# Out-projection ahead of the scores in every slot of a fused attention and feed-forward block

## The chip, the cores and the metric

The kernel runs on one core of a Trainium2 chip. The metric is the device time of one execution in microseconds; the time before is the median of three runs. The chip's engines have short names here, as in the profile: PE is TensorE (matmuls; PEld are its weight loads), DVE is VectorE, ACT is ScalarE, POOL is GpSimd, and SP is the engine whose queue issues most DMAs. Each engine works through its own instructions in the order in which they were written down, and waits at an instruction until the semaphores that it names have arrived.

## The reference

One transformer block on x of shape (2, 1024, 256), all in fp32. A small modulation gives each batch entry a shift, a scale and a gate for both halves of the block. Cut to what matters here:

```python
h = layernorm(x) * (1 + ca) + sa
q, k, v = h @ Wq + bq, h @ Wk + bk, h @ Wv + bv      # 16 heads of 128
q, k = rotary(q * 128 ** -0.5), rotary(k)
attn = softmax(causal(q @ k.T))                      # 1024 x 1024 for each batch entry and head
x = x + ga * ((attn @ v) @ Wo + bo)
h = layernorm(x) * (1 + cb) + sb
x = x + gb * ffn(h)                                  # silu(gate) * up, down; hidden size 704
```

## The kernel before

The attention is a loop over 32 **units** (2 batch entries x 8 head groups x 2 heads), numbered 0 to 31 by `n`, and in each unit over 8 **slots** `i`, one for each block of 128 query rows. The whole order is written out by hand (`tc.manual_schedule()`): each engine executes its instructions in the order in which this loop names them, and only semaphores tie the engines together.

In slot i of a unit the kernel computes, for query block i:

- `score` (L380): one or two fp32 matmuls per block, (i+1) x 128 columns wide in all, from `qT` and `kT` into the PSUM tile `ps` (L392). Every fp32 matmul appears as two passes in the trace. Then one DVE instruction adds the causal mask and finds the negative row maximum `nmax` (L395, with a second short row that reads the accumulator).
- `turned` (L422): DVE transposes the exponentials of the slot **before** (i-1) in 32x32 squares into `t32` (L426). Slot 0 does so for the last block of the unit before. After blocks 3 and 7, SP issues 16 DMAs (L438) that move the squares into `pT`, the transposed probabilities of four blocks.
- `expo` (L407): ACT computes exp(ps - max) from PSUM and the row sums `den` (L412).
- `project_out` (L472): for an earlier unit whose attention output `o` is complete, one matmul of 256 columns, `py` (L479), and on DVE the sum of x, x = py * rden + x (L482). In slots 0 to 3 it takes rows 4 to 7 of unit n-2, in slots 4 to 7 rows 0 to 3 of unit n-1. In slots 0 and 4 a reciprocal of four row sums (L476) stands ahead of it on DVE.
- `release` (L375): the second half of a rotary embedding (L365 on DVE, L368 on POOL) of a projection that was made in the slot before.
- One more piece of TensorE work: in slots 1, 3, 4 and 6 a projection of q or k for the next unit (`project_qk`, L349; ACT's L361 and POOL's L362 follow), in slots 0 and 2 a projection of v (`project_v`, L331, copied out of PSUM by ACT), in slots 5 and 6 `values` (L453), the product with v of blocks 4 to 7 of the unit before, and in slot 7 the same for blocks 0 to 3 of this unit.
- `extras` (L545): small pieces that belong to certain units, such as layer-norm statistics (units 13 and 28), the scaling and turning of normalised rows by TensorE transposes (L201, L210, L217; units 14, 15, 30, 31) and scaling of feed-forward weights.

In unit 31, which has no next unit, slots 1 to 6 carry matmuls of the feed-forward (`hidden`, L508) in place of projections. After the loop come the last out-projections and the rest of the feed-forward.

What matters for the order is which buffers each piece shares. PSUM is divided among `ps` (two buffers, `ps_sc`), `py` (**one** buffer, `ps_y`), `po` (one buffer, `ps_o`) and the projections (two buffers, `ps_a`). A matmul into a buffer waits until the last reader of what lay in it is done: `py` waits for the L482 before it, `ps` for the exponential two slots back, `po` for ACT's copy of `o`. `pT` has one buffer for each half of a unit; its copies wait for the `po` matmuls that read the last contents, and `po` waits for the copies to land.

Of the kernel before, what the change touches and what calls it, by code (L numbers as in the profile page):

```python
# [37 lines left out]
def adaln_block(ctx: ExitStack, tc: tile.TileContext, a, cos_d, sin_d, out):  # L38
# [24 lines left out]
    def load_x(b, t, n, eng):  # L63
        eng.dma_start(x[b][:, t : t + n, :], x_d[b, :, t : t + n, :])
# [123 lines left out]
    def ln_sqrt(b, name, t0, t1):  # L188
        mv, rstd = stats[b, name]
        nc.scalar.activation(rstd[:, t0:t1], mv[:, t0:t1, 1], AF.Sqrt, bias=eps_t)  # L190
# [79 lines left out]
    def new_hT(b, blk):  # L270
        hT[b, blk] = hpool.tile([P, KC, QB], F32, tag=f"hT{blk}", name=f"hT{b}_{blk}")
        return hT[b, blk]

    def load_w(b, g, n):
        t = wpool.tile([P, KC, HG * DH], F32, tag=f"w{n}", name=f"w{n}_{b}{g}")
        nc.sync.dma_start(
            t, a[f"L0_attn_W{n}"][g]
        )
        weights[b, g][n] = t

    def load_proj(b, g):
        weights[b, g] = {}
        for n in ("q", "k", "v"):
            load_w(b, g, n)

    def load_out(b, g):
        t = wpool.tile([P, HG, D], F32, tag="wo", name=f"wo_{b}{g}")
        nc.sync.dma_start(
            t, a["L0_attn_Wo"][g]
        )  # L290
        weights[b, g]["o"] = t
# [88 lines left out]
    def score(u, i):  # L380

        b, g, h = u
        tag = f"{b}{g}{h}{i}"
        qT, kT = qks[u, "q"], qks[u, "k"]
        L = (i + 1) * P
        if i == 0:
            dens[u] = small.tile([P, NT], F32, tag="den", name=f"den_{tag}", bufs=3)
            rdens[u] = small.tile([P, NT], F32, tag="rden", name=f"rden_{tag}", bufs=3)
        ps = ps_sc.tile([P, S], F32, tag="sc", name=f"ps_{tag}")
        for c in range(0, L, 512):  # L390
            e = min(L, c + 512)
            nc.tensor.matmul(ps[:, c:e], qT[:, ts(i, P)], kT[:, c:e], start=True, stop=True)  # L392

        nmax = small.tile([P, 1], F32, tag="nmax", name=f"nmax_{tag}")
        nc.vector.tensor_tensor_reduce(  # L395
            ps[:, :L],
            ps[:, :L],
            mask[:, NT - 1 - i :, :].rearrange("p t k -> p (t k)"),
            -SCALE,
            FLT_MAX,  # L400
            ALU.add,
            ALU.min,
            nmax,
        )
        return ps, nmax
# [60 lines left out]
    def bank(name):  # L466

        pool, tag = banks[turn[0] % 4]
        turn[0] += 1
        return pool.tile([P, 512], F32, tag=tag, name=name)  # L470

    def project_out(u, t, late=False):  # L472

        b, g, h = u
        if t % 4 == 0:
            nc.vector.reciprocal(rdens[u][:, t : t + 4], dens[u][:, t : t + 4])  # L476
        name = f"py_{b}{g}{h}{t}"
        py = bank(name) if late else ps_y.tile([P, 512], F32, tag="y", name=name)
        nc.tensor.matmul(  # L479
            py[:, :D], outs[u][:, ts(t, P)], weights[b, g]["o"][:, h, :], start=True, stop=True  # L480
        )
        nc.vector.scalar_tensor_tensor(  # L482
            x[b][:, t, :], py[:, :D], rdens[u][:, t : t + 1], x[b][:, t, :], ALU.mult, ALU.add
        )
# [57 lines left out]
    units = [(b, g, h) for b in range(B) for g in range(NG) for h in range(HG)]  # L542
# [52 lines left out]
    with tc.manual_schedule():  # L595
        nc.scalar.activation(
            sc.rearrange("p b k -> p (b k)"), sc.rearrange("p b k -> p (b k)"), AF.Silu
        )
        nc.scalar.activation(warm, eps_t, AF.Sqrt)
        weights[0, 0] = {}  # L600
        load_w(0, 0, "q")
        load_w(0, 0, "k")
        for t, t_d in ((cos_t, cos_d), (sin_t, sin_d)):
            nc.sync.dma_start(t[:, :QB], t_d[:, :QB])
        load_w(0, 0, "v")
        for t in (4, 6):
            load_x(0, t, 2, nc.sync)
        for t, t_d in ((cos_t, cos_d), (sin_t, sin_d)):
            nc.sync.dma_start(t[:, QB:], t_d[:, QB:])
        nc.sync.dma_start(wga, a["w_gates"])  # L610
        nc.sync.dma_start(wmod[:, 1], a["L0_wmod"][1])
        load_proj(*units[2][:2])
        load_out(0, 0)
        nc.gpsimd.memset(bvacc, 0.0)

        for blk, t in enumerate(t32):
            for j in range(3):
                nc.gpsimd.memset(t[:, :, j, 4 * blk + j + 1 :, :], 0.0)
        for t in (0, 2):
            for j in range(2):  # L620
                ln_stats(0, "a", t + j)
            ln_sqrt(0, "a", t, t + 2)
            if t:
                ln_scale(0, "a", 0, (0, 1))
        modulation(0, ps_y, "y")
        ln_scale(0, "a", 0, (2, 3))
        shift_scale(0)
        ln_turn(0, "a", 0, 0, new_hT(0, 0), split=True)
        for t in range(4, NT):
            ln_stats(0, "a", t)  # L630
        ln_sqrt(0, "a", 4, NT)
        for s in ("q", "k"):
            project_qk(units[0], s, 0)
        for t in (0, 2):
            project_v(0, 0, t, *((ps_o, "o"), (ps_y, "y"))[t // 2])
        ln_scale(0, "a", 1)
        release()
        ln_turn(0, "a", 1, 0, new_hT(0, 1), split=True)
        gates()
        for s in ("q", "k"):  # L640
            project_qk(units[0], s, 1)
        nc.gpsimd.dma_start(bo_bc, a["L0_attn_bo"].to_broadcast([P, D]))

        for n, u in enumerate(units):
            b, g, h = u
            prev = units[n - 1] if n else None
            nxt = units[n + 1] if n + 1 < N else None
            nb, ng = (b, g + 1) if g + 1 < NG else (b + 1, 0)
            more = nb < B
            for i in range(NT):  # L650
                ps, nmax = score(u, i)
                if i >= 1:
                    turned(u, i - 1)
                elif prev:
                    turned(prev, NT - 1)
                expo(u, i, ps, nmax)

                if i < 4 and n > 1:
                    project_out(units[n - 2], 4 + i)
                if i >= 4 and prev:  # L660
                    project_out(prev, i - 4)
                release()
                if i in (1, 3, 4, 6) and nxt:
                    project_qk(nxt, *{1: ("q", 0), 3: ("k", 0), 4: ("q", 1), 6: ("k", 1)}[i])
                if i in (5, 6) and prev:
                    values(prev, 1, 4 * (i - 5), 4 * (i - 4))

                if i == 7 and prev:
                    values(u, 0, 0, 4)
                if n == 1 and i == 1:  # L670
                    values(prev, 0, 0, 4)
                if i in (0, 2):
                    if h == 0:
                        project_v(b, g, 4 + i)
                    elif more:
                        project_v(nb, ng, i)
                if not nxt and 1 <= i < 7:
                    hidden(0, 0, i - 1, late=False)
                extras(n, i)
                if i == 7 and h == 1:  # L680
                    if more:
                        load_out(nb, ng)
                    if n + 3 < N:
                        load_proj(*units[n + 3][:2])

        u, prev = units[-1], units[-2]
        turned(u, 7)
        for c in range(4):
            hidden(0, 1, c)
            project_out(prev, 4 + c, late=True)  # L690
            project_out(u, c, late=True)
        values(u, 1, 0, 8)
        hidden(0, 1, 4)
        for t in range(4, NT):
            project_out(u, t, late=True)
        hidden(0, 1, 5)
        for t in range(NT):
            ln_stats(1, "b", t)
        ln_sqrt(1, "b", 0, NT)
        down(0, 0, 0)  # L700
        ln_scale(1, "b", 0)
        down(0, 0, 1)
        down(0, 0, 2)
        ln_turn(1, "b", 0, 2, new_h2(1, 0))
        down(0, 0, 3)
        ln_scale(1, "b", 1)
        for c in range(NF):
            hidden(1, 0, c)
            if c == 0:
                ln_turn(1, "b", 1, 2, new_h2(1, 1))  # L710
            if c in (1, 2, 3, 4):
                down(0, 1, c - 1)
        for c in range(NF):
            hidden(1, 1, c)
            if c in (1, 2, 3, 4):
                down(1, 0, c - 1)
        for j in range(4):
            down(1, 1, j)
# [68 lines left out]
```

## Time and profile before

| What | Value |
|---|---|
| Median of 3 runs | 1104.93 us (1104.89 to 1105.02) |
| The profiled execution: its time / its span | 1106.62 us / 1104.9 us |
| Granted TensorE clock over the span | 0.998 |
| PE `ps` L392, `po` L453, `py` L479: busy, instructions | 289.7 us x768, 263.3 us x768, 157.2 us x512 |
| DVE maximum L395, transpose L426, sum of x L482: busy, instructions | 195.7 us x256, 198.2 us x256, 115.9 us x256 |
| ACT exponential L412: busy, instructions | 189.7 us x256 |
| `pT` copies L438 on SP's queue: issues of 128 KB and of 64 KB | x512, x512 |

How to read it: the span runs from the first to the last instruction of the profiled execution; the execution's own time has a little around it. A group's row gives busy time, count and mean duration. A row of the timeline gives the start in us from the span's start, the duration in us, then engine, line, operation and tiles; "[0.35 <-DVE x L482]" at its end is the idle time of the engine before it and what ended it. A row "xN" merges N neighbours, and its duration runs from the first one's start to the last one's end. Matmuls are pipelined, so the row of one is longer than the distance to the next. In a table of waits, a row names who waited for whom, the total in us, how often, and the longest. A row of the table by stretches gives the stretch, its length, the busy time and count of PE, PEld, DVE, ACT and POOL, the granted TensorE clock (1.00 is full), the share of the DMA engines and GB/s.

### The profile page before, as it was taken

How to read it: one execution, taken by the hardware profiler on the slowest of the kernel's cores; microseconds unless marked ns; L12 is line 12 of the kernel's file. 1: busy time of each engine (PE TensorE's matmuls, PEld its weight loads, DVE VectorE, ACT ScalarE, POOL GpSimd, SP SyncE). 2: the span in 40 equal slices, each digit the busy share in tenths (PEclk: the TensorE clock that was granted, in tenths of full speed). 3: DMA queues.
4: the chain of work that ended last, by engine and by line, in shares of the span. 5: the costliest groups of instructions: out<-in, count | busy, mean ns of one | idle time of the engine just before them, and what ended most of it. 6: DMA issues, size and time to landing. Idle time of an engine off the chain costs nothing.

```text
span 1104.9 us, 12352 instructions
## 1 busy us (share of the span) xinstructions
PE 1092.1 (99%) x3556; PEld 645.3 (58%) x3556; DVE 643.0 (58%) x1406; ACT 508.5 (46%) x953; POOL 391.8 (35%) x356
## 2 busy tenths in 40 slices
PE   9999999999999999999999999999999999999998
PEld 5555555555666565555555656656565555455555
DVE  5556565666566666865566566555656757544311
ACT  5644444554555445354454455444444454641110
POOL 4635353535353433444333543333433433000000
PEclk9999999999999999999999999999999999999999
DMA  6365656556556655265654546454545455331000
GB/s 213 83 146 126 162 117 167 144 119 146 127 144 143 146 112 134 65 145 115 142 125 110 143 110 145 108 143 109 139 101 139 97 118 115 85 79 32 24 19 29
DMA packets 65656, 128.88 MB, mean 117 GB/s; under 512 B 18451, under 2 KB 22803, under 8 KB 65589
## 3 DMA queue, kind: packets, MB, share of 16 engines
q1 hardware_dynamic: 63236, 123.81, 47.5%
q10 hardware_dynamic: 2304, 4.16, 1.1%
q8 instruction: 29, 0.48, 0.2%
q14 instruction: 39, 0.31, 0.1%
q0 software_dynamic: 48, 0.13, 0.1%
HBM read 25.26 MB, written 2.10 MB: 25 GB/s over the span
## 4 chain that ended last, share of the span: by engine, by line
PE 97%; DVE 3%; issue 0%; ACT 0%; POOL 0%; DVEq 0%; ACTq 0%; POOLq 0%
PE ps L392 22%; PE po L453 22%; PE py L479 10%; PE pq L349 10%; PE pk L349 10%; PE pv L331 9%; PE pgu L508 7%; PE pd L530 4%; DVE t L426 1%; PE warm_ps L82 1%; DVE ps L395 1%; PE pm L119 0%; PE ptx_a L210 0%; DVE x L482 0%; DVE kT L365 0%
## 5 line engine op out<-in xcount | busy, mean ns | idle before, releaser
L395 DVE CUSTOM_DVE_ANT_0 ps<-ps,mask 128x128 f32<-128x128 f32 (+7 forms) x256 | 195.7, 764 | 328.9 <-PE ps L392 328.5
L412 ACT ACTIVATE p<-ps,nmax 128x128 f32<-128x128 f32 (+7 forms) x256 | 189.7, 741 | 345.8 <-DVE nmax L395 342.4
L392 PE MATMUL ps<-kT,qT 128*128 128x512 f32 (+3 forms) x768 | 289.7, 486 | 0.7 <-ACT p L412 0.7
L453 PE MATMUL po<-pT,v 128*128 128x512 f32 (+3 forms) x768 | 263.3, 486 | 0.0
L392 PEld LDWEIGHTS ps<-kT,qT 128*128 128x128 f32 x768 | 140.9, 190 | 127.2 <-issue 120.8
L453 PEld LDWEIGHTS po<-pT,v 128*128 128x128 f32 x768 | 145.9, 190 | 115.4 <-issue 91.8
L426 DVE STREAM_TRANSPOSE t<-p 128x128 f32<-128x128 f32 (+7 forms) x256 | 198.2, 774 | 1.0 <-ACT p L412 0.7
L479 PE MATMUL py<-wo,o 128*128 128x256 f32 x512 | 157.2, 391 | 1.5 <-DVE x L482 1.5
L362 POOL TENSOR_TENSOR r_k<-r_k,sin_t 128x512 f32<-128x512 f32 x64 | 81.3, 1271 | 209.8 <-ACT r_k L361 209.7
L368 POOL TENSOR_TENSOR kT<-kT,r_k 128x512 f32<-128x512 f32 x64 | 81.5, 1273 | 162.7 <-DVE kT L365 148.3
L362 POOL TENSOR_TENSOR r_q<-r_q,sin_t 128x512 f32<-128x512 f32 x64 | 81.8, 1277 | 150.8 <-ACT r_q L361 147.1
L479 PEld LDWEIGHTS py<-wo,o 128*128 128x128 f32 x512 | 90.0, 190 | 61.2 <-issue 30.9
L331 PE MATMUL pv<-wv,hT 128*128 128x256 f32 x512 | 120.9, 379 | 1.1 <-DVE qT L365 1.1
L349 PE MATMUL pq<-hT,wq 128*128 128x512 f32 x256 | 120.6, 593 | 0.5 <-DVE hT L217 0.5
L482 DVE SCALAR_TENSOR_TENSOR x<-py,rden,x 128x256 f32<-128x256 f32 x256 | 115.9, 455 | 8.0 <-DVE rden L476 0.9
L349 PE MATMUL pk<-hT,wk 128*128 128x512 f32 x256 | 120.3, 592 | 0.0
L361 ACT ACTIVATE r_q<-pq,cols 64x512 f32<-64x512 f32 x128 | 87.4, 683 | 48.1 <-PE pq L349 47.2
L331 PEld LDWEIGHTS pv<-wv,hT 128*128 128x128 f32 x512 | 97.1, 190 | 15.2 <-DVE qT L365 1.2
L361 ACT ACTIVATE r_k<-pk,cols 64x512 f32<-64x512 f32 x128 | 87.4, 683 | 18.0 <-PE pk L349 15.9
L368 POOL TENSOR_TENSOR qT<-qT,r_q 128x512 f32<-128x512 f32 x64 | 83.7, 1308 | 25.3 <-DVE qT L365 20.7
L349 PEld LDWEIGHTS pk<-hT,wk 128*128 128x128 f32 x256 | 48.6, 190 | 35.8 <-issue 32.0
L349 PEld LDWEIGHTS pq<-hT,wq 128*128 128x128 f32 x256 | 48.3, 190 | 35.7 <-issue 31.2
(83 smaller groups left out, 704.6 us busy)
## 6 DMA issues: line engine op xcount, KB each, us to landing
pT<-t SPq DMA_DIRECT2D x512, 128.0 KB, 2.4
pT<-t SPq DMA_DIRECT2D x512, 64.0 KB, 2.0
wq<-in_Wq SPq DMA_DIRECT2D x16, 256.0 KB, 3.0
wk<-in_Wk SPq DMA_DIRECT2D x16, 256.0 KB, 4.1
wv<-in_Wv SPq DMA_DIRECT2D x16, 256.0 KB, 4.3
wo<-in_Wo SPq DMA_DIRECT2D x16, 256.0 KB, 2.9
out<-yo SPq DMA_DIRECT2D x16, 128.0 KB, 1.7
x<-in_x SPq DMA_DIRECT2D x4, 256.0 KB, 5.1
```

The costliest lines, as they stand in the source:

```text
L331: nc.tensor.matmul(pv[:, ts(j, HG * DH)], hT[b, n][:, k, ts(r, P)], weights[b, g]["v"][:, k, :], start=(k == 0), stop=(k == KC - 1),)
L349: nc.tensor.matmul(pq, weights[b, g][s][:, k, ts(h, DH)], hT[b, n][:, k, :], start=(k == 0), stop=(k == KC - 1),)
L361: nc.scalar.activation(r1[to], pq[of], AF.Identity, bias=cols[of, c : c + 1])
L362: nc.gpsimd.tensor_tensor(r1, r1, sin_t[:, sl], ALU.mult)
L368: nc.gpsimd.tensor_tensor(dst[:, sl], dst[:, sl], r1, ALU.add)
L392: nc.tensor.matmul(ps[:, c:e], qT[:, ts(i, P)], kT[:, c:e], start=True, stop=True)
L395: nc.vector.tensor_tensor_reduce(ps[:, :L], ps[:, :L], mask[:, NT - 1 - i :, :].rearrange("p t k -> p (t k)"), -SCALE, FLT_MAX, ALU.add, A ...
L412: nc.scalar.activation(p[:, :L], ps[:, :L], AF.Exp, bias=nmax, scale=-1.0, accum_out=dens[u][:, i : i + 1])
L426: nc.vector.transpose(t32[blk][:, :, j, : i + 1, :].rearrange("p c k b -> p k c b"), p[:, : (i + 1) * P].rearrange("p (k c a) -> p k c a", ...
L453: nc.tensor.matmul(po[:, off * P :], vs[b, g][:, k, ts(h, DH)], pT[:, off:, :, k, :], start=(k == 0), stop=(k == last),)
L479: nc.tensor.matmul(py[:, :D], outs[u][:, ts(t, P)], weights[b, g]["o"][:, h, :], start=True, stop=True)
L482: nc.vector.scalar_tensor_tensor(x[b][:, t, :], py[:, :D], rdens[u][:, t : t + 1], x[b][:, t, :], ALU.mult, ALU.add)
```

## The change

`project_out` moves from behind `expo` to the front of the slot. On PE the order of a slot becomes `py`, `ps`, the slot's further piece, where it was `ps`, `py`, further piece. On DVE it becomes the sum of x (in slots 0 and 4 with its reciprocal), the maximum, the transpose, the release, where it was the maximum, the transpose, the sum, the release. ACT, POOL and SP keep the order of their own instructions, and no instruction is added or removed. Which rows are projected in which slot stays the same, and so do all buffers.

```diff
@@ -648,17 +648,17 @@
             for i in range(NT):
+
+                if i < 4 and n > 1:
+                    project_out(units[n - 2], 4 + i)
+                if i >= 4 and prev:
+                    project_out(prev, i - 4)
                 ps, nmax = score(u, i)
                 if i >= 1:
                     turned(u, i - 1)
                 elif prev:
                     turned(prev, NT - 1)
                 expo(u, i, ps, nmax)
-
-                if i < 4 and n > 1:
-                    project_out(units[n - 2], 4 + i)
-                if i >= 4 and prev:
-                    project_out(prev, i - 4)
                 release()
                 if i in (1, 3, 4, 6) and nxt:
                     project_qk(nxt, *{1: ("q", 0), 3: ("k", 0), 4: ("q", 1), 6: ("k", 1)}[i])
```

## The prediction

> **What bounds the kernel now.** I read the page first: busy time, then the chain that ended last.
>
> ```profile
> PE 1092.1 (99%) x3556; PEld 645.3 (58%) x3556; DVE 643.0 (58%) x1406; ACT 508.5 (46%) x953; POOL 391.8 (35%) x356
> ...
> PE 97%; DVE 3%; issue 0%; ACT 0%; POOL 0%; DVEq 0%; ACTq 0%; POOLq 0%
> ```
>
> TensorE carries 97% of the chain. A change of order adds no matmul, so only its waits can be won or lost. "Busy" hides short ones, because each matmul row is longer than the distance to the next. I therefore took distances from start to start. Next, the table of waits (total, times, longest), with TensorE's two rows on `py`:
>
> ```profile
> PEld py L479 <- DVE x L482: 8.7, 30, 1.2
> ...
> PE py L479 <- DVE x L482: 1.5, 3, 0.8
> ```
>
> The out-projection waits for the sum of x (L482) some 30 times, about once a unit: `py` has one PSUM buffer, which the sum before it must empty. The timeline of TensorE, at the seam of two units (slot 0 of unit 10 begins at 312.24), shows the price:
>
> ```profile
> 312.24 0.39 PE L392 MATMUL ps<-kT,qT 128*128 128x128 f32 x2
> 312.53 0.70 PE L479 MATMUL py<-wo,o 128*128 128x256 f32 x2
> 313.07 1.89 PE L331 MATMUL pv<-wv,hT 128*128 128x256 f32 x8
> 314.79 0.59 PE L392 MATMUL ps<-kT,qT 128*128 128x256 f32 x2
> 315.23 0.67 PE L479 MATMUL py<-wo,o 128*128 128x256 f32 x2
> 315.74 1.88 PE L349 MATMUL pq<-hT,wq 128*128 128x512 f32 x4
> 317.45 0.81 PE L392 MATMUL ps<-kT,qT 128*128 128x384 f32 x2
> 318.10 0.59 PE L479 MATMUL py<-wo,o 128*128 128x256 f32 x2
> 318.53 0.38 PE L331 MATMUL pv<-wv,hT 128*128 128x256 f32 x1
> ```
>
> In slot 2, `py` takes 318.53-318.10 = 0.43. In slot 0 it takes 0.54, in slot 1 0.51, and slot 0's score takes 0.29, where the same 128-wide pair takes 0.22 in slot 4 (324.12 to 324.34). Lost per unit: 0.07+0.11+0.08 = 0.26 us. The timeline of DVE says why:
>
> ```profile
> 311.00 1.11 DVE L426 STREAM_TRANSPOSE t<-p 128x896 f32<-128x896 f32 x1
> 312.04 0.44 DVE L482 SCALAR_TENSOR_TENSOR x<-py,rden,x 128x256 f32<-128x256 f32 x1
> 312.40 0.74 DVE L365 SCALAR_TENSOR_TENSOR kT<-pk,cols,cos_t 128x512 f32<-128x512 f32 x1
> 313.05 0.29 DVE L395 CUSTOM_DVE_ANT_0 ps<-ps,mask 128x128 f32<-128x128 f32 x1
> 313.26 0.14 DVE L395 DVE_READ_ACCUMULATOR2_ANT nmax<- 128x1 f32 x1
> 313.26 1.24 DVE L426 STREAM_TRANSPOSE t<-p 128x1024 f32<-128x1024 f32 x1
> 314.42 0.13 DVE L476 RECIPROCAL rden<-den 128x4 f32<-128x4 f32 x1
> 314.66 0.48 DVE L482 SCALAR_TENSOR_TENSOR x<-py,rden,x 128x256 f32<-128x256 f32 x1
> ```
>
> Slot 7's sum ends at 312.48, behind the maximum and a 1.11 transpose; slot 0's at 315.14, behind a 1.24 one. `py` starts 0.05 and 0.09 later.
>
> **What the change removes.** With `py` first, slot 7's sum starts when its `py` is done, near 308.6 (`py` at 307.94), and DVE is free then: its next maximum begins at 309.86 before. Slot 0's sum comes ahead of the 1.24 transpose. From 310.29 (slot 7's maximum, 0.43 later than 309.86, since `py` now precedes the score), DVE's start-to-start steps are: maximum 1.14, transpose 1.04, L365 0.65, reciprocal 0.24; the sum starts at 313.36 and ends at 313.80. Slot 1's `py` wants its weights from 314.4. Both waits go. 26 units (2 to 13, 16 to 28, 30) x 0.26 = 6.8. Units 14 and 29 lose more, because the last two layer-norm statistics instructions of the unit before stand in DVE's queue: slot 1's score at 432.87 is followed by `py` at 433.82, 0.95 where 0.43 is due, so 0.52+0.26 = 0.78 each. There the new sum ends near 432.4, just as its `py` becomes due: I take 1.5 for the two. **Removed: 8.3.**
>
> [...] The weight-load timeline has `py`'s loads starting with the wait's end (312.53, 315.20), and the passes 0.11 and 0.08 too long. The row decides: 6.8.
>
> **What it delays.** The score, maximum and exponential of a slot move back by one `py`, 0.43. The score two slots on needs the exponential's PSUM buffer: slot 7's exponential ends at 312.44, and slot 1's score starts at 314.79, so 2.3 of cover; 0.43 is free. The rotary part L365 moves 0.43-0.36 = 0.07; its bank, given back at 320.24, is wanted at 321.55. ScalarE's copies are queued behind the exponential: the `po` copy at 312.44 moves to about 312.9, and its bank is wanted at slot 5. No DMA is issued by the moved code, and POOL's order is unchanged.
>
> SP is reached indirectly. Slot 0's transpose now has the reciprocal and the sum ahead of it: 0.24+0.40, less the 0.36 of slot 7's sum, plus the 0.43: 0.71 later. The 16 copies of `pT`, queued on SP behind it, feed slot 5's `po`:
>
> ```profile
> 314.56 10.02 SPq L438 DMA_DIRECT2D pT<-t  x16
> ```
>
> Issue starts 0.06 after the transpose ends (314.50). The last lands at 326.39, 1.81 after its issue ended; `po` starts at 328.21 and its weight load 0.21 earlier. Transpose's end to `po` is 13.71, so the reserve is 13.71-0.06-10.02-1.81-0.21 = 1.61. It loses 0.71, and 0.26 since TensorE comes earlier: 0.64 stays, and a typical unit loses nothing. But single issues, mostly 0.59, last up to 1.98, and then 16 take longer. In the same view the batches for units 4, 13, 23 and 28 took 11.42, 10.92, 11.38 and 10.75. With 10.66 allowed, units 4 and 23 would be 0.76 and 0.72 late. At 13 and 28, where 0.78 is won and the transpose moves 0.74, 10.11 is allowed: 0.81 and 0.64 late. Sum 2.9. Which batch is hit is chance: between 0 and about 5 (seven of 29 batches at 0.7). I take 2.9, what this trace's batches give. The batches of slot 4 have 2.1 and lose 0.43: no cost.
>
> **Two seams with TensorE transposes.** In slot 0 of unit 15 TensorE waits for a bank (0.96 until 467.35) that ScalarE's `v` copy frees, queued behind the exponential of slot 0. DVE's reciprocal and sum (0.64) and the 0.07 now stand ahead of that maximum: the bank comes about 0.9 later than 467.35 at 468.25; then transposes 0.49, `py` 0.43, score 0.43 give 469.60 for the next projection, 469.14 before: +0.5. In unit 31 the bank freed by L217 at 946.15 comes about 0.13 later; then slot 2's maximum stands behind the feed-forward product and now also the sum (0.36), with the activation-table reloads behind it and 0.17 of cover: +0.25. Together **+0.9**.
>
> **The clock.** Behind unit 31's waits the granted clock halved:
>
> ```profile
> 941.90:945.30 3.40, 1.52 (x8) 0.94 (x8) 3.30 (x7) 0.46 (x2) 1.05 (x1) 1.00 0.00 0
> 945.90:949.30 3.40, 3.40 (x6) 1.47 (x5) 1.90 (x6) 0.56 (x2) 0.00 (x0) 0.53 0.93 206
> ```
>
> The first number after the stretch's length is TensorE's busy time; the 1.00 and 0.53 are the clock. Three matmuls took 0.85 to 0.9 instead of 0.43, 1.4 in all. [...] no single gap here exceeds 1.3, [...] by the row a stretch busy for under half is enough. Unit 15's gap grows to about 1.8, with TensorE busy for about half of 3.4. Unknown: from -1.4 (unit 31 escapes) to +1.4 (unit 15 falls too). I take +0.7, half of the event, as its stretch lies between the one that fell and what it was (2.23 busy of 3.4, no fall).
>
> **Sum.** -8.3 +2.9 +0.9 +0.7 = -3.8. The profiled execution's span is 1104.9 (1106.62 with what lies around it); the median of the runs is 1104.93, the span again, so I subtract from the median: **1101.1**.
>
> **Rivals.**
> - *The copies stay hidden* (few long issues, no second clock fall): -8.3+0.9 = -7.4, 1097.5. For it: 27 batches had the cover. Against: long issues occur throughout the trace.
> - *Another wait eats it* (no effect): the waits at `py` return at `po` or the exponential. It takes 0.26 in every unit, or half that with both clock events: about 1105. Against: 0.64 and 2.3 of cover.
> - *Slower: the `pT` copies become late in every unit.* Place: `po` in slot 5. The loss is 28 x (x-0.64), x being the further delay of the last landing. It cancels the net removal of 7.4 at x = 0.90 and is 0.2% slower from 0.98, which 0.06 more per issue would do; x = 1.2 gives 1113. For it: 13.71 is a chain of 17 steps through one queue. Against: nothing in the change lengthens an issue.
>
> **How the numbers follow.** Part of the gain kept (1098.5 to 1102.7): 0.62. Hidden copies: 0.15. Eaten: 0.12. Slower: 0.11. What a measurement of this kernel can tell from no change is about 0.2%, 2.2 us; below 1102.7 is faster. Faster 0.77, same 0.12, slower 0.11. The range runs from 1097.0, just under the hidden-copies case, to 1105.0, where 5 of late copies and both clocks leave nothing; it leaves out 0.2.
>
> **What would show it.** Right: the wait of `py` for L482 under 2; seam slots with `py` at 0.43; most units 29.26 instead of 29.52 long; the last transpose to `po` 12.74, longer only behind slow batches; L482 now waiting for `py` on DVE at no cost. Wrong: `po` waiting for DMA in most units, `ps` waiting for the exponential, or a second stretch of half clock elsewhere.

## The result, and the profile after

The changed kernel takes **1102.12 us** in the median of 8 executions (1099.5 to 1102.94), where the kernel before, beside it, takes 1104.97 (8 executions, 1104.74 to 1105.36). The ratio is 0.9969, 95% interval 0.9959 to 0.998: faster by 0.3%, a little more than a measurement of this kernel can tell. The forecast was 1101.1, range 1097 to 1105. The profiled execution of the changed kernel took 1102.0, its span is 1100.2; before, they were 1106.62 and 1104.9. From profile to profile the change of the span is -4.7, from median to median it is -2.85, and much of what follows is about the difference between these two.

From the page of the changed kernel: busy time, the chain that ended last by engine, and two groups (line, engine, operation, tiles, count | busy, mean ns | idle time of the engine before them).

```profile
PE 1086.2 (99%) x3556; PEld 645.8 (59%) x3556; DVE 658.5 (60%) x1406; ACT 504.3 (46%) x953; POOL 391.1 (36%) x356
...
PE 97%; DVE 2%; DMA 0%; issue 0%; ACT 0%; POOL 0%; DVEq 0%; ACTq 0%; POOLq 0%
...
L453 PE MATMUL po<-pT,v 128*128 128x512 f32 (+3 forms) x768 | 263.6, 486 | 1.1 <-DMA pT<-t 1.1
L482 DVE SCALAR_TENSOR_TENSOR x<-py,rden,x 128x256 f32<-128x256 f32 x256 | 123.0, 482 | 183.0 <-PE py L479 176.0
```

TensorE remains the bound at 97% of the chain. "DMA" has come into the chain, with a share that rounds to nothing, and the third row names it: 1.1 us in which `po` waited for the copies of `pT`. The last row is the sum of x, before which DVE now stands idle for 183 us, nearly all of it until `py` is done. The table of waits of the changed kernel (total, times, longest):

```profile
DVE x L482 <- PE py L479: 176.0, 135, 2.4
DVE ps L395 <- PE ps L392: 131.2, 180, 3.1
...
PEld py L479 <- DVE nmax L395: 7.7, 32, 0.2
```

Before, `py` waited for the sum of x in 33 places, up to 1.2 us in one. These rows are gone. What is left for `py`'s weight load is 7.7 in 32 places, none over 0.2, and put down to the maximum, which stands behind the sum. The next view shows what such a row is worth. DVE's new waits for `py` cost nothing by themselves: DVE is not what the end waits for.

The timeline of TensorE in the changed kernel, at the same seam of units 9 and 10 as in the prediction:

```profile
310.20 0.60 PE L479 MATMUL py<-wo,o 128*128 128x256 f32 x2
310.64 0.38 PE L392 MATMUL ps<-kT,qT 128*128 128x128 f32 x2
310.86 1.89 PE L331 MATMUL pv<-wv,hT 128*128 128x256 f32 x8
312.59 0.59 PE L479 MATMUL py<-wo,o 128*128 128x256 f32 x2
313.02 0.59 PE L392 MATMUL ps<-kT,qT 128*128 128x256 f32 x2
313.45 1.88 PE L349 MATMUL pq<-hT,wq 128*128 128x512 f32 x4
315.17 0.59 PE L479 MATMUL py<-wo,o 128*128 128x256 f32 x2
```

From start to start, `py` takes 0.44 in slot 0 (310.64-310.20) and 0.43 in slot 1, where it took 0.54 and 0.51; slot 0's score takes 0.22 (0.29). All three losses are gone, so the waits of 0.2 listed for `py` lie under the matmul before it. The same place on DVE:

```profile
310.43 0.71 DVE L365 SCALAR_TENSOR_TENSOR kT<-pk,cols,cos_t 128x512 f32<-128x512 f32 x1
311.06 0.16 DVE L476 RECIPROCAL rden<-den 128x4 f32<-128x4 f32 x1
311.33 0.48 DVE L482 SCALAR_TENSOR_TENSOR x<-py,rden,x 128x256 f32<-128x256 f32 x1
311.73 0.29 DVE L395 CUSTOM_DVE_ANT_0 ps<-ps,mask 128x128 f32<-128x128 f32 x1
311.93 0.14 DVE L395 DVE_READ_ACCUMULATOR2_ANT nmax<- 128x1 f32 x1
311.93 1.24 DVE L426 STREAM_TRANSPOSE t<-p 128x1024 f32<-128x1024 f32 x1
```

The sum of slot 0 is done at 311.81, 0.78 before slot 1's `py` begins. The reciprocal and the sum now stand ahead of slot 0's transpose, which ends at 313.17. Its 16 copies are issued by SP from 313.24; the second row is the same batch for unit 13, which met long issues:

```profile
313.24 10.03 SPq L438 DMA_DIRECT2D pT<-t  x16
...
430.86 11.18 SPq L438 DMA_DIRECT2D pT<-t  x16
```

The typical batch still takes 10.03 and costs nothing. Behind the one of 11.18, in unit 14, the product waits:

```profile
444.13 3.67 PE L453 MATMUL po<-pT,v 128*128 128x512 f32 x8 [0.94 <-DMA pT<-t]
```

Start to start, that wait costs 1.18; behind the batches of units 23 and 28 it is 0.25 and 0.40: 1.83 in all, and nothing in the other units. Unit 28's batch was issued in nearly the usual time (10.13); its last copy landed 2.23 after its issue ended, where about 1.8 is usual.

Last the table by stretches (length, then busy time and count of PE, PEld, DVE, ACT and POOL, the granted clock, DMA share, GB/s) behind unit 31's waits:

```profile
939.00:942.00 3.00, 2.41 (x4) 0.84 (x3) 2.76 (x7) 0.31 (x1) 0.00 (x0) 0.50 0.44 96
942.00:945.00 3.00, 3.00 (x5) 1.35 (x4) 0.00 (x0) 1.25 (x3) 0.00 (x0) 0.50 0.95 210
```

The clock is at 0.50 in both. Before, it was halved in one such stretch at the same place (0.53). The matmuls here lose 2.8 by it, before 1.4.

Where the 4.7 went, by the lengths of the units from score to score, and within units 14, 15, 29 and 31 by TensorE's start-to-start distances against those of an unhindered matmul of the same width:

| | forecast | profile to profile |
|---|---|---|
| waits at `py` and the score removed (units 2 to 14 and 16 to 30) | -8.3 | -8.0 |
| `po` behind late copies (units 14, 24, 29) | +2.9 | +1.8 |
| seams of units 15 and 31 without the clock | +0.9 | +0.3 |
| half clock | +0.7 | +1.35 |
| sum | -3.8 | -4.6 (spans: -4.7, both to rounding) |

A plain unit is 29.273 long, from score to score, and was 29.521.

### The profile page after: what moved, and what is told of

Read it like the earlier page. It is cut to its first block, busy times and chain, and to the rows that moved or that the text cites. A ratio compares the mean times of both kernels' runs of the same rounds, so it can differ in the third digit from the quotient of the medians.

```text
span 1100.2 us, 12351 instructions
## 1 busy us (share of the span) xinstructions
PE 1086.2 (99%) x3556; PEld 645.8 (59%) x3556; DVE 658.5 (60%) x1406; ACT 504.3 (46%) x953; POOL 391.1 (36%) x356
## 4 chain that ended last, share of the span: by engine, by line
PE 97%; DVE 2%; DMA 0%; issue 0%; ACT 0%; POOL 0%; DVEq 0%; ACTq 0%; POOLq 0%
PE ps L392 22%; PE po L453 22%; PE pq L349 10%; PE pk L349 10%; PE py L479 10%; PE pv L331 10%; PE pgu L508 7%; PE pd L530 4%; PE warm_ps L82 1%; DMA pT<-t 0%; PE pm L119 0%; PE ptx_a L210 0%; DVE t L426 0%; DVE ps L395 0%; PE ptx_b L210 0%
## 5 line engine op out<-in xcount | busy, mean ns | idle before, releaser
L482 DVE SCALAR_TENSOR_TENSOR x<-py,rden,x 128x256 f32<-128x256 f32 x256 | 123.0, 482 | 183.0 <-PE py L479 176.0
L392 PEld LDWEIGHTS ps<-kT,qT 128*128 128x128 f32 x768 | 145.7, 190 | 77.5 <-issue 63.1
L479 PE MATMUL py<-wo,o 128*128 128x256 f32 x512 | 151.4, 380 | 0.0
L479 PEld LDWEIGHTS py<-wo,o 128*128 128x128 f32 x512 | 92.5, 190 | 65.2 <-issue 52.1
```

Source lines behind the costliest of these rows:

```text
L479: nc.tensor.matmul(py[:, :D], outs[u][:, ts(t, P)], weights[b, g]["o"][:, h, :], start=True, stop=True)
L482: nc.vector.scalar_tensor_tensor(x[b][:, t, :], py[:, :D], rdens[u][:, t : t + 1], x[b][:, t, :], ALU.mult, ALU.add)
```

## The experiments

The experiments use the same kernel, with `project_out` cut into its matmul (`out_mm`) and its DVE part (`out_sum`, with the reciprocal), and `score` into its matmuls and the maximum (`row_max`), so that each can be placed alone. Their line numbers differ from the page above: maximum L400, transpose L431, `po` L458, `py` L486, reciprocal L492, sum of x L498. The slot of the changed order reads, in this form:

```python
py = out_mm(*who) if who else None     # who: the earlier unit and row block, as before
if who:
    out_sum(*who, py)
ps = score(u, i)
nmax = row_max(u, i, ps)
turned(...)                            # block i-1
expo(u, i, ps, nmax)
release()
```

**The two kernels again.** First the kernel before, unchanged, and the changed order in the form above.

> The unchanged kernel of before, profiled again. The profiled execution of before took 1106.62, its timed runs 1104.97 in the median, 1.65 less. Theory: that one execution was slow by the half clock of unit 31 (1.4), which most executions don't have. Then this profile has an execution near 1105.0, a span near 1103.2, and no stretch at half clock behind unit 31, or 1106.6 with one. Rival: the half clock is in every execution and the profile adds 1.65 for itself; then the span is 1104.9 again, with the half clock, and timed runs at 1105.0.

> The changed order once more, written with the out-projection split in its matmul and its sum (same instructions in the same order). If the spread of the changed kernel's runs (1099.5 to 1102.9) comes from which batches of pT copies are slow and from half-clock stretches, this profile has units of 29.27 wherever the batch was quick, a wait of po for the copies behind each batch of more than about 10.7, and times between 1099 and 1103. Rival: a longer period in all units in the slower executions.

The kernel before took 1105.26 (13 executions; the same kernel in the series' own comparison 1105.97, 52 executions). Its profiled execution took 1105.16, span 1103.4, 1.5 less than the one that the prediction was made from, and the table by stretches shows why. Behind unit 31's waits, in this execution:

```profile
945.00:948.00 3.00, 2.52 (x7) 1.16 (x7) 2.77 (x7) 0.56 (x2) 0.00 (x0) 1.00 0.66 146
```

The clock stays at 1.00 where it was 0.53 in the profile that the prediction shows. The stretch of half clock belongs to some executions and not to others. Their times show it without a profile. Of 83 executions of the kernel before in this and the later series, the 47 with a mean clock of 0.999 or above took 1104.81 to 1105.75 (median 1105.18), the 36 at 0.998 or below 1106.18 to 1108.25 (median 1106.62); nothing lies between. The median of 1104.93 that the forecast started from is of the first kind, the profiled execution with 1106.62 of the second.

The changed order again took 1102.83 (7 executions, 1099.87 to 1104.1; ratio 0.9968, 0.9955 to 0.998). Units are 29.273 long again. `po` waits behind four slow batches (0.85, 1.38, 0.36, 1.01 in units 5, 14, 24, 29), 3.6 in all. In this execution the clock falls at both seams, in unit 15 and behind unit 31:

```profile
468.00:471.00 3.00, 3.00 (x5) 1.41 (x5) 1.43 (x5) 0.56 (x2) 0.00 (x0) 0.50 0.97 212
...
942.00:945.00 3.00, 2.77 (x6) 1.40 (x7) 3.00 (x7) 0.46 (x2) 0.00 (x0) 0.53 0.21 44
```

Unit 15 is 34.33 long with the fall and 32.63 without. The result repeats, the waits of `po` vary from execution to execution, and the half clock has a second place.

**One slot only.** The new order in slot 7 alone, all other slots as before.

```diff
-                py = out_mm(*who) if who else None
-                if who:
-                    out_sum(*who, py)
+                if i == 7:
+                    py = out_mm(*who) if who else None
+                    if who:
+                        out_sum(*who, py)
                 ...
                 expo(u, i, ps, nmax)
+                if i < 7 and who:
+                    project_out(*who)
```

> Only slot 7 begins with its out-projection; slots 0 to 6 keep the old order. Theory (one chain on DVE from slot 7's maximum to slot 0's sum sets both waits): slot 0's loss of 0.18 goes, but slot 0's sum still stands behind the 1.24 transpose and ends 0.07 later, so slot 1's loss grows from 0.08 to about 0.33. Period 29.52 to 29.6, time 1105 to 1107: no gain. Rival (two independent waits): 0.18 less in 28 units, 5.0 less, 1100.

It took 1106.71 (21 executions; ratio 1.0014, 1.0007 to 1.002), with units of 29.565. TensorE's timeline at the seam:

```profile
312.50 0.39 PE L392 MATMUL ps<-kT,qT 128*128 128x128 f32 x2
312.72 0.60 PE L486 MATMUL py<-wo,o 128*128 128x256 f32 x2
313.15 1.89 PE L331 MATMUL pv<-wv,hT 128*128 128x256 f32 x8
314.88 0.59 PE L392 MATMUL ps<-kT,qT 128*128 128x256 f32 x2
315.50 0.70 PE L486 MATMUL py<-wo,o 128*128 128x256 f32 x2
316.04 1.45 PE L349 MATMUL pq<-hT,wq 128*128 128x512 f32 x3
```

Slot 0 has no loss any more: score 0.22, `py` 0.43. But slot 1 has all of it: score 0.62 where 0.43 is due, `py` 0.54, together 0.30. Slot 0's sum still stands behind the 1.24 transpose, and TensorE arrives earlier. The two waits are one chain through DVE; freeing its first link alone hands the wait to the second.

**Only DVE's order.** TensorE as before (score, then `py`), DVE as in the changed kernel (sum, maximum, transpose).

```diff
+                ps = score(u, i)
                 py = out_mm(*who) if who else None
                 if who:
                     out_sum(*who, py)
-                ps = score(u, i)
                 nmax = row_max(u, i, ps)
```

> TensorE keeps the old order (scores, then out-projection); only on DVE does the sum stand ahead of the maximum. Theory: the waits at py go all the same (period 29.27), so the order on DVE makes the gain; but slot 7's maximum now also waits for its py and sum, the last transpose is about 1.1 later than before instead of 0.71, and the copies' reserve falls from 0.64 to about 0.25: more units wait at po, 1 to 2.5 slower than the changed kernel, 1102 to 1105. Rival (TensorE's order makes the gain): period 29.52, 1105 or more.

It took 1106.32 (22 executions; ratio 1.0005, 0.9999 to 1.0011), 1.3 above the upper end of what was expected. The units are 29.273 long, so the order on DVE is what removes the waits at `py`. But none of the gain is left. From its page:

```profile
L458 PE MATMUL po<-pT,v 128*128 128x512 f32 (+3 forms) x768 | 264.1, 487 | 4.4 <-DMA pT<-t 2.5
```

That is not the half clock alone: the 7 executions at a mean clock of 0.999 or above have a median of 1105.56, where the kernel before has 1105.18. `po` now waits for copies in nine units, 6.5 in total, start to start, and in this profile units 15 and 31 take 1.8 more than in the kernel before at full clock. The sum waits for a `py` that comes a score later, and the transpose behind it waits too: from its end to `po` there are 12.37, against 12.75 in the changed kernel. What TensorE's half of the change is for is this: with `py` first, the sum's wait is over before the score is, and delays nothing.

**Only TensorE's order.** `py` first, but the sum of x behind the maximum and the transpose, as before.

```diff
                 py = out_mm(*who) if who else None
-                if who:
-                    out_sum(*who, py)
                 ps = score(u, i)
                 ...
                 expo(u, i, ps, nmax)
+                if who:
+                    out_sum(*who, py)
```

> Only TensorE's order is changed: each slot begins with the out-projection's matmul, but on DVE the sum stays behind the maximum and the transpose. Theory (DVE's order makes the gain): py now wants its buffer 0.2 to 0.4 earlier while the sums that free it come later (slot 7's at 312.9 for a py due at 312.2, slot 0's at about 315.9 for one due at 315.4): about 1.2 to 1.4 lost per unit at py, period near 30.6, 1132 to 1140. Rival (TensorE's order makes the gain): as the changed kernel, 1102.

It took 1169.32 (2 executions; ratio 1.0574, 1.0555 to 1.0594): the direction as expected, the size twice that. The table of waits:

```profile
PEld py L486 <- DVE x L498: 116.0, 148, 1.4
...
PE py L486 <- DVE x L498: 42.8, 92, 1.2
```

2.38 are lost in each unit, in four slots (0, 1, 4 and 5), where the expectation had reckoned with two seams only. `py` comes a whole score earlier, and the sum that must empty its one buffer stands behind a maximum and a transpose in DVE's queue. Each half of the change alone gives nothing or costs; the gain comes from both together.

**The reserve of the `pT` copies.** The changed order with three additional DVE instructions, whose results nothing uses, ahead of slot 0's transpose.

```diff
                 nmax = row_max(u, i, ps)
+                if i == 0 and n > 1:
+                    for j in range(3):
+                        st = small.tile([P, 6], F32, tag="st", name=f"late_{n}_{j}")
+                        nc.vector.bn_stats(st, mask[:, 2 * j : 2 * j + 2, :].rearrange("p t k -> p (t k)"))
```

> The changed order with three additional statistics instructions on DVE (about 1.2 in all, results unused) right ahead of slot 0's transpose. Theory (copies' reserve of 0.64 behind a chain of transpose, 16 copies and po): the reserve becomes -0.6, po waits for the copies in every unit, the transpose-to-po distance stops falling at about 12.1, period about 29.8 and more behind slow batches: 20 to 23 more, 1121 to 1126. Rival (the copies have more cover than I reckoned): unchanged, 1102 to 1104.

It took 1119.32 (2 executions; ratio 1.0122, 1.0104 to 1.0141), 1.7 below the lower end of what was expected. On DVE's timeline the three stand where they were meant to, and begin 0.99 before the transpose, where 1.2 had been reckoned:

```profile
316.20 1.07 DVE L680 BATCH_NORM_STATS2 late<-mask 128x6 f32<-128x256 f32 x3
317.19 1.23 DVE L431 STREAM_TRANSPOSE t<-p 128x1024 f32<-128x1024 f32 x1
```

The group of `po` on its page reads:

```profile
L458 PE MATMUL po<-pT,v 128*128 128x512 f32 (+3 forms) x768 | 265.5, 489 | 12.8 <-DMA pT<-t 9.9
```

`po` is now late in every unit but the 15th, which has waits of its own: 0.3 to 0.8 in most units, 1.4 to 2.2 in units 10, 14, 24 and 29, 19.7 in all. This is the slower rival of the forecast, brought about on purpose. With 0.99 more delay and 0.3 to 0.8 of it lost in most units, between 0.2 and 0.7 of reserve were left there in the changed kernel; 0.64 had been reckoned.

**Giving some reserve back.** The changed order with both reciprocals of a unit made in slot 3, so that none stands ahead of slot 0's transpose.

```diff
                 if who:
-                    out_sum(*who, py)
+                    out_sum(*who, py, early=True)      # no reciprocal here
                 ...
                 release()
+                if i == 3 and prev:
+                    recip(prev, 0)
+                    recip(prev, 4)
```

> The changed order, with the two reciprocals of a unit both made in slot 3, so that none stands ahead of slot 0's transpose. Theory (the transpose's delay is what uses up the reserve of the pT copies): the transpose ends 0.24 earlier, so the distance from its end to po is 12.99 instead of 12.75, and the waits of po fall from 1.8 to 3.6 in total to 0.9 to 2.2; no other wait changes, and the seams and the clock stay as in the changed order: 0.7 to 1.5 below the changed order in this series. Rival (the waits of po are set by the long issues alone): waits of po unchanged, and the time of the changed order within 0.3.

It took 1100.73 (5 executions, 1098.71 to 1100.92), and the changed order beside it 1101.53: 0.8 less. From the transpose's end to `po` there are now 13.04, and `po` waits 1.84 in this profile, 2.26 in the one beside it. Both lie inside what the theory gave, but a difference of 0.4 in the waits is smaller than what they vary by between executions (1.8 to 3.6 for the changed order). The size of this effect rests on the distance alone: the intervals of the two ratios (0.9938 to 0.9963, and 0.995 to 0.9977 for the changed order beside it) overlap as well.

**The seams and the clock.** The changed order, with the old one in slot 0 of unit 15 and in all of unit 31; then with only one of the two; and the changed order itself a third time.

```diff
+                if i == 0 and n == 15 or n == 31:      # or one of the two alone
+                    ps = score(u, i)
+                    nmax = row_max(u, i, ps)
+                    turned(...)
+                    expo(u, i, ps, nmax)
+                    if who:
+                        project_out(*who)
+                else:
                     ...
```

> The changed order, but slot 0 of unit 15 and all of unit 31 keep the old one. Executions of the changed kernel at a mean clock of 0.999 or 1.000 took 1099.5 to 1100.8, those at 0.996 to 0.998 mostly 1102.0 to 1104.1; of before 1105 and 1106.6. Theory: the longer TensorE gaps at these two seams bring the half-clock stretches, one or two in most executions. Then this one has as many as before (none or one): 1100 to 1101.5 in the median, and no half clock in unit 15. It also gains some 0.3 at the seams. Rival: stretches of half clock fall by chance whatever the order; then 1102 to 1103, with clocks of 0.997 as often.

> The changed order again, as the comparison for the next three. Theory (the order itself is worth 5 us, and stretches of half clock at the seams of units 15 and 31 take back about 2): 1101 to 1103, over half of the executions at a mean clock of 0.998 or below, those at 0.999 or above at 1099.5 to 1100.8. Rival (the changed order brings no more such stretches than the order before; the earlier runs were chance): as many as of the kernel before, about half, and 1100.5 to 1101.5.

> The changed order, with the old one in slot 0 of unit 15 only. If the additional stretches of half clock come from unit 15's longer gap, this removes those (1.3 to 1.5 in the executions that have one) and the 0.1 to 0.2 of the seam, and leaves those behind unit 31 (up to 1.35 to 2.8): 1100.8 to 1101.8. If they all come from unit 31, it takes the time of the changed order less 0.2. If neither seam matters, likewise.

> The changed order, with the old one in all of unit 31 only. If the stretches behind unit 31 are the dearer ones (2.8 of excess in the changed order's profile where the order before had 1.4 or none), this takes 1100.3 to 1101.3, with fewer executions at 0.998 or below than the changed order has. If unit 15 is the dearer one, 1101.5 to 1102.5.

| | time | ratio, 95% interval | executions at a mean clock of 0.998 or below |
|---|---|---|---|
| before | (1105.18 at full clock) | 1 | 36 of 83 |
| changed order, three series | 1102.12, 1102.83, 1101.53 | 0.9969, 0.9968, 0.9964 | 14 of 20 |
| old order in unit 15's slot 0 | 1101.69 | 0.9963 (0.995 to 0.9975) | 4 of 5 |
| old order in unit 31 | 1100.99 | 0.9955 (0.9943 to 0.9968) | 4 of 5 |
| old order in both | 1100.46 | 0.995 (0.9937 to 0.9964) | 2 of 5 |

With both seams old, the time is 1.1 to 2.4 below those of the three changed series, as expected, and the profile has no half clock at the seams. With one of them, 4 of 5 executions have one all the same (fewer had been expected with unit 31's seam old), so that neither seam alone is the cause. The profiles show three places. In the third changed series it is unit 15, here with the stretch ahead of the fall:

```profile
462.00:465.00 3.00, 1.76 (x10) 1.18 (x8) 2.90 (x7) 0.19 (x1) 1.62 (x2) 1.00 0.00 0
465.00:468.00 3.00, 2.20 (x8) 1.94 (x9) 2.51 (x4) 0.74 (x3) 0.00 (x0) 0.62 0.33 71
468.00:471.00 3.00, 3.00 (x9) 1.70 (x8) 1.01 (x4) 0.82 (x3) 0.00 (x0) 0.81 0.96 213
```

That makes unit 15 1.6 longer (34.24). With unit 15's seam old it fell behind unit 31 (0.51 from 939 to 942). With unit 31's old it fell in neither, but at the very beginning, where no part of this change is:

```profile
6.00:12.00 6.00, 5.74 (x34) 4.71 (x33) 3.87 (x14) 1.09 (x3) 0.00 (x0) 0.75 1.02 368
```

The theory that the changed order has more of these stretches agrees with the counts (14 of 20 against 36 of 83); single executions at 0.996 and 0.995 (1102.0 to 1103.55) have more or longer ones than the kernel before shows. The counts do not settle the share of each place: five executions for each arrangement are too few, and the beginning takes part.

**All of it together.** Reciprocals in slot 3, slot 0's transpose ahead of its maximum, and the old order at both seams.

```diff
                     ps = score(u, i)
+                    if i == 0 and prev:
+                        turned(prev, NT - 1)
                     nmax = row_max(u, i, ps)
-                    turned(...)
+                    if i:
+                        turned(u, i - 1)
```

> The changed order with a shorter way to the last transpose: both reciprocals moved into slot 3, slot 0's transpose ahead of slot 0's maximum, and the old order (maximum, transpose, sum) in slot 0 of unit 15 and in unit 31. Theory: the transpose comes 0.24 and about 0.25 earlier, the reserve rises from 0.64 to about 1.1, only batches above 11.2 are late: the 1.8 to 3.6 of waits at po fall below 1; with the seams as in the run that keeps their old order 1098.5 to 1100. Rival: slot 0's exponential, now 1.2 later, becomes a wait at slot 2's scores or v's bank, and it is slower than that run.

It took **1097.32** (5 executions, 1096.71 to 1098.44; ratio to the kernel before 0.9925, 0.9912 to 0.9937), 1.2 better than expected and faster than both kernels. From the transpose's end to `po` there are 13.25, and on its page the group of `po` has no DMA in front any more:

```profile
L458 PE MATMUL po<-pT,v 128*128 128x512 f32 (+3 forms) x768 | 263.6, 486 | 0.5 <-issue 0.5
```

Start to start `po` still loses 1.37 (0.73 in unit 14, 0.21 in units 11, 24 and 29), though the slow batches are there: 11.19, 11.41 and 10.75 for units 13, 23 and 28. All five executions ran at a mean clock of 0.999 or above, so against the kernel before at full clock (1105.18) the gain is 7.9, or 0.7%. That none of the five has a half-clock stretch may in part be luck. What the transpose ahead of the maximum gives by itself was not tried.

## Why the prediction was right, and where it was off

The forecast was that part of a gain of 8.3 would be kept, and so it went: faster, and inside the range. Step by step:

- **What is removed** (-8.3) came out at -8.0, and for the reason given. The losses of `py` behind its weight loads, 0.11 and 0.08, were rightly counted in: with the score's loss of 0.07 alone only 26 x 0.07 = 1.8 would have gone. The trace of the changed kernel has 0.25 less in each of 26 units and 0.8 less in units 14 and 29; the missing 0.3 is that a plain unit is 29.273 long and not 29.26. That DVE's order does it, and that the two waits are links of one chain, is shown by the two experiments on slot 7 and on DVE's order.
- **Late copies** (+2.9, range 0 to 5): 1.8, 3.6 and 2.3 in three executions. The distance from transpose to `po` is 12.75 where 12.74 was forecast, and the slow batches came behind the same units as before (13 and 23 in all three, 28 and 4 in some), so "chance" was too strong a word for where they fall; how long they take does vary. (The forecast's list left out a fifth slow batch of the profile before, 11.19 for unit 14; unit 15 is long enough to cover it.) Slow issues are not the only cause: two of the ten waits stand behind a batch issued in the usual time whose last copy landed 2.23 and 3.11 after its issue, where the forecast took 1.81 as fixed. The experiment that spent the reserve bears it out: `po` was then late in nearly every unit.
- **Seams** (+0.9): about +0.3. In unit 15 the later bank cost 0.15 instead of 0.5, because the waits of `py` and of the projection behind it, 0.7 before, went at the same time, and the working had kept part of them. In unit 31, 0.15 instead of 0.4.
- **The clock** (+0.7, -1.4 to +1.4): +1.35 from profile to profile. Ahead of the fall in unit 15 (0.62 from 465 to 468 in the third changed series) TensorE was busy for 1.76 of 3 us. The longest gap between two matmuls in that unit is 1.64 in the first profile of the changed kernel, where the clock stays at 1.00 there (it was 0.96 before, and 1.8 was forecast). The forecast's reading, that a stretch busy for under half is enough, does not hold: in the second profile of the kernel before, TensorE is busy behind unit 31 for the same 1.52 us between 942 and 945 as in the first, then for 2.52 against 2.51 to 948, and the clock there is 1.00 and not 0.62. What separates the two was not shown. Unit 15's fall, named as a possibility, occurs in two of three profiles.
- **The step that failed is the last one: "the median is the span again, so I subtract from the median".** The two are not of one kind. An execution is 1.7 longer than its span (1106.62 and 1104.9; 1102.0 and 1100.2), and the profiled execution of before held a stretch of half clock that the median lacked. The likeness of 1104.9 and 1104.93 was an accident of +1.7 and -1.7. The working had both numbers and the row with the 0.53 in front of it; one should have asked what the median would show of that row. Taken from the execution's own 1106.62, the same sum gives 1102.8, and 0.9 of that is the size of the terms above; the measured 1102.12 lies between the two. Two errors of opposite sign, 1.7 in the base and 0.9 in the sum, brought the forecast within 1.0 of the measured time: that closeness is luck.

Compared at equal clock, the change is clearer. At 0.999 or above the changed order takes 1099.5 to 1100.88 (6 executions, median 1100.08), the order before 1105.18: **-5.1**. At 0.998 or below the medians are 1102.65 and 1106.62: -4.0. The median of the result, -2.85, is smaller than both because it sets an execution with a half-clock stretch (after) against one without (before). Equal clocks leave out that the changed order has the stretch more often; over all executions on record, 20 and 83, the medians are 1102.15 and 1105.41: -3.3.

Of the rivals, "the copies stay hidden" (1097.5) falls with the waits of `po`, although single executions came within 2 of it. "Another wait eats it" is what happened to the order on DVE alone: 6.5 of late copies, and 1106.32. The slower rival needed 0.90 more delay to cancel the gain by its working; with 0.99 more the kernel was 1.2% slower. Its formula gives 28 x (0.99-0.64) = 9.8 of loss there, and 19.7 was measured: one reserve for all units leaves out the slow batches and the units that have less.

## What to carry to other kernels

Where one buffer is emptied by an engine with a long queue, look at the place of the emptying instruction in that queue, not only at that of the matmul that fills it: DVE's order alone brought the units from 29.521 to 29.273 here, and TensorE's alone lost 2.38 in each. But moving it forward pays only if what it waits for comes early enough (DVE's order alone lost 6.5 to late copies), so move both, and count what each of them now stands ahead of. Ask what the next chain has in reserve before giving its time away: here it was 0.64 of 13.7, late transfers used it up in three or four units of each profile, and the version that gave 0.5 back and left the two critical seams alone took the gain from 0.3 or 0.4% to about 0.7%. And compare like with like: a profiled execution with an event in it must be held against executions that have that event, or the event taken out.

## What the runs showed that had not been expected

- The kernel before has two times, 1.4 us apart (1105.18 and 1106.62 in the median), with nothing between 1105.75 and 1106.18, and which of them an execution takes goes with a single stretch of a few us at half clock. In the profiles of both orders and their variants the stretch comes at one of three places with waits on TensorE: at the very start (0.75 from 6 to 12), in unit 15 (0.50 from 468 to 471), behind unit 31 (0.50 from 939 to 945). No gap in unit 15 or behind unit 31 is longer than 1.64 us in the first profiles of the two orders; the longest one of the kernel before is 1.3, behind unit 31.
- What decides whether it comes was not shown. The waits and TensorE's busy time alone do not tell it: behind unit 31 in the kernel before, the busy times of the two profiles are the same to 0.01, and the clock from 945 to 948 is 0.62 in one and 1.00 in the other. In unit 15 of the changed order, 1.36 busy of 3 us (465 to 468, second series) were followed by 3 us at 0.50, and 1.39 (462 to 465, first profile) by 3 us at 1.00.
- The slow batches of `pT` copies recur at the same units in kernels with different orders (13, 23 and 28 in nearly every profile, 4 in about half), at 10.7 to 11.6 where 10.03 is usual. That they recur speaks against chance; what sets them was not shown.
- Units 14 and 29 have almost no reserve. Without its wait of 1.18, `po` in unit 14 would come 12.15 after the transpose's end, not 12.75, since the layer-norm instructions of the unit before stand in DVE's queue ahead of that transpose. The forecast had allowed 10.11 for the copies' issue there, and the batch of 11.18 in the changed kernel, 1.07 more, cost 1.18.
